# A graph network kernel on one core: products of zeros ahead of the first loads, another second product, and the first sums on VectorE

## The chip, the core and the metric

The kernel runs on one core of a Trainium2 chip. The metric is device time in microseconds of one execution, the median over several. Beside the timed runs there is one profiled execution, and all views of the profile are of that one. The engines are TensorE (PE; its weight loads are shown as PEld), VectorE (DVE), ScalarE (ACT), GpSimd (POOL) and SyncE (SP), which issues most DMAs here.

## The reference

128 graphs of 128 nodes with 512 features each pass two layers, all in fp32. With `x` of shape (128, 128, 512) and `adj` of (128, 128, 128):

```
deg = sum(adj, -1)
agg = (adj @ x) / max(deg, 1e-6)
x   = layernorm(x + relu(concat(x, agg) @ W.T))          # layer 0, W is (512, 1024)
h   = relu(adj @ (x @ W1) + b1)
h   = relu(adj @ (h @ W2) + b2)
x   = layernorm(x + adj @ (h @ W3) + b3)                 # layer 1, W1..W3 are (512, 512)
```

## The kernel before, in words

Four graphs make a quad; there are 32 quads. Within a quad a product of 512 rows by a 512x512 weight is cut into 2x2 blocks and done in Strassen-Winograd fashion: 7 block products instead of 8, with sums of blocks of the data and of the weight made beforehand by other engines. From the third quad on, the products are cut a second time in the same way (`inner_product`, L617). The first two quads use one level in layer 0 (`product`, L599, four fp32 matmuls of 128x128 by 256 columns; the trace shows each as two records).

The two halves of the first weight are called WB (it multiplies x to give `y`, which `adj` then aggregates, L916) and WA (it multiplies x directly). Both live in the tile `big`. The first quad's transposed x lives in the tile `T1` (in the profile `T`), the second quad's in `xT`. Each holds seven places, one for each of the seven products: places 0, 1, 2, 3, 4, 5, 6 belong to products 1, 7, 6, 5, 2, 4, 3. The operands of products 1 and 2 are raw blocks on both sides. The other five take a sum on at least one side:

- `Data.sums` (L446) makes the places 3, 2, 1 and 6 of x from its four loaded blocks (places 0, 1, 4, 5). By default it asks for GpSimd, with VectorE as a substitute; with `at_end=True` for VectorE alone.
- `Weight.__init__` (L343) loads four blocks of a weight into four places, and `Weight.sums` (L349) makes the other three, on VectorE, and puts a fourth difference in the place of a loaded block.

`wino_a` (L775) issues the first five of the seven products, `wino_b` the last two. The order in `wino_a` is 1, 5, 6, 2, 7. In the first quad (`key[1]` is 0) the copy of product 1, which ScalarE makes, is added to the bank of product 2 by VectorE; in the others the bank is seeded with it.

No instruction is issued where it stands in the program. Each is recorded in `Plan` with an estimated duration, the keys that it reads and writes, and the buffers that it takes. `Plan.deadlines` gives TensorE's operations due times in the order in which they are recorded, and the others due times from those. `Plan.order` then plays the engines in time with the estimates and takes for each engine the most urgent operation that is ready (for TensorE the first ready one of the next 48). So the order of all engines' work, the DMAs on SP's queue included, follows from the recorded order of the products: a load that an earlier product needs gets an earlier due time. What is emitted directly, as the memset of `eps` (L1244), stands ahead of the plan.

Once both halves of the first weight have been used by the first quad, `to_forms` (L377) writes the 49 inner blocks of each to DRAM (`forms`), and from the third quad on `Streamed.parts` (L425) loads the blocks of both halves again into a ring of six buffers, three of them in `big`. The degrees of the first quad go through DRAM on ScalarE's queue (`degrees`, L550): `dd`, then `ah`; the row of degrees also gates the loads of W1, W2 and W3.

Of the kernel before, what the change touches and what calls it, by code (L numbers as in the profile page):

```python
# [14 lines left out]
P = 128  # L15
# [228 lines left out]
def gnn_resnorm_kernel(  # L244
# [15 lines left out]
    nc = tc.nc  # L260
    NG, F = x.shape[0], 512
# [12 lines left out]
    def tile_of(shape, name):  # L274
        return sbuf.tile(shape, F32, tag=name, name=name)

    BANK = [psum.tile([P, 2, H], F32, tag=f"bank{i}", name=f"bank{i}") for i in range(8)]
    S_T = [tile_of([P, 2, H], f"s{i}") for i in range(NS)]
# [7 lines left out]
    AT_T = [tile_of([P, G, P], f"at{i}") for i in range(2)]  # L286
# [22 lines left out]
    def pinned(ins):  # L309
        return tc.keep_in_program_order(ins)  # L310

    def vector(n, emit, reads, writes, shared=False, lead=None):
        plan.op("DVE", 0.06 + 0.00123 * n, emit, reads, writes, shared, lead=lead)
# [4 lines left out]
    def dma(dst, src, reads, writes, size, queue="SP", lead=None):  # L318
        eng = nc.sync if queue == "SP" else nc.scalar
        plan.op(queue, 0.06, lambda: pinned(eng.dma_start(dst(), src())), reads, writes, size=size, lead=lead)  # L320

    def const(v):
        return lambda: v

    def add(eng, n, dst, a, b, reads, writes, op=OP.add, shared=False, lead=None):

        on_vector = lambda: pinned(nc.vector.tensor_tensor(dst(), a(), b(), op=op))  # L327
        if eng == "POOL":
            on_gpsimd = lambda: pinned(nc.gpsimd.tensor_tensor(dst(), a(), b(), op=op))  # L329
            plan.op("POOL", 0.03 + 0.00243 * n, on_gpsimd, reads, writes, True, other=(0.06 + 0.00123 * n, on_vector), lead=lead)  # L330
        else:
            vector(n, on_vector, reads, writes, shared)
# [5 lines left out]
    class Weight:  # L338
# [4 lines left out]
        def __init__(self, name, w, after=()):  # L343
            self.name, self.t, self.ti = name, W_T[name], WI_T.get(name)
            wv = w.rearrange("(h c p) (o n) -> p h o c n", p=P, c=2, o=2)
            for i, j, k in ((0, 0, 0), (0, 1, 3), (1, 1, 6), (1, 0, 4)):
                dma(const(self.t[:, k]), const(wv[:, i, j]), after, [(name, k)], P * 2 * H * 4)

        def sums(self):  # L349
            for d, a, b in ((1, 6, 3), (3, 3, 0), (2, 6, 3), (5, 4, 2)):  # L350
                add(
                    "DVE", F, const(self.t[:, d]), const(self.t[:, a]), const(self.t[:, b]),
                    [(self.name, a), (self.name, b)], [(self.name, d)], OP.subtract, True,
                )
# [156 lines left out]
    X0, X1 = Data("T1", T_T[1]), Data("xT", XT_T)  # L511
# [22 lines left out]
    def load_xt(q):  # L534
        d = xa(q)
        for h in range(2):
            for ms in ((0,), (1,)) if q == 0 else ((0, 1),):
                dma(
                    const(d.t[:, 4 * h + ms[0] : 4 * h + ms[-1] + 1]), const(xT[q][:, h, ms[0] : ms[-1] + 1]),
                    (), d.keys([4 * h + m for m in ms]), P * F * 4 * len(ms),  # L540
                )
# [26 lines left out]
    def bank_ap(s):  # L568
        return BANK[s.index]
# [7 lines left out]
    def copied(p, n=4):  # L577
        s = Slot("s")
        scalar(n * P, lambda: pinned(nc.scalar.copy(quarters_of(s, n), quarters(p, n))), [p], [s])  # L579
        return s  # L580

    def seeded(p, n=4):

        s = Slot("bank", n * P, seeded=True)
        scalar(n * P, lambda: pinned(nc.scalar.copy(quarters(s, n), quarters(p, n))), [p], [s])  # L585
        return s

    def product(p, a, b, k, start, transposed):
        (ta, ka), (tb, kb) = a.block(k), b.block(k)

        def emit():
            for o in range(2):
                for c in range(2):
                    if transposed:
                        lhsT, rhs = tb[:, c, o * P : (o + 1) * P], ta[:, c].rearrange("p g n -> p (g n)")
                    else:
                        lhsT, rhs = ta[:, c, o, :], tb[:, c, :]
                    r = pinned(
                        nc.tensor.matmul(  # L599
                            bank_ap(p)[:, o, :], lhsT, rhs, start=start and o == 0 and c == 0, stop=c == 1,  # L600
                            skip_group_check=True,
                        )
                    )
            return r

        plan.op("PE", 1.728, emit, ka + kb, [p])
# [168 lines left out]
    def wino_a(key, a, b, c00, c11, transposed=False):  # L775

        py, pz = Slot("bank"), Slot("bank")
        product(py, a, b, 1, True, transposed)
        px = seeded(py) if key[1] else Slot("bank")
        s1 = None if key[1] else copied(py)  # L780
        yield
        product(pz, a, b, 5, True, transposed)
        yield
        product(py, a, b, 6, False, transposed)
        s2 = copied(py)
        yield
        product(px, a, b, 2, not key[1], transposed)
        if s1 is not None:
            add("DVE", F, lambda: bank_ap(px), lambda: bank_ap(px), lambda: S_T[s1.index], [px, s1], [px])
        c00(px)  # L790
        yield
        product(py, a, b, 7, False, transposed)
        s3 = copied(py)
        c11(s3, pz)
        yield
        CHAIN[key] = py, pz, s2
# [20 lines left out]
    def rows_a(key, a, b, t):  # L817
        yield from wino_a(key, a, b, copy_to(t, 0, 0), sums_to(t, 1, 1))
# [176 lines left out]
    def seg_h1_a(q):  # L995
        d = data(q, "h1")
        yield from wino_a(("h1", q), data(q, "g1"), W1, lambda p: relu_to(d, 0, p), sums_h1(q, 1, 1), transposed=True)
# [188 lines left out]
    def seg_last(q, m):  # L1186
# [51 lines left out]
        for j, o in enumerate(os):  # L1238
# [2 lines left out]
                [o], [("out", q, m, j)], P * F * 4,  # L1241
            )

    nc.vector.memset(EPS_T, LN_EPS)  # L1244
    load_xt(0)
    WB = Weight("wb", w0T[F : 2 * F])
    X0.sums()
    WB.sums()
    load_adj(0)
    degrees(0)  # L1250
# [146 lines left out]
```

## Time and profile before

| | us |
|---|---|
| median of 3 timed runs | 2249.04 (2248.91 to 2249.4) |
| profiled execution | 2250.41 |
| its span, first to last instruction | 2248.5 |
| first matmul starts | 5.46 |
| last matmul ends | 2242.2 |

The profiled execution is 1.9 us longer than its span, and 1.4 us longer than the median of the timed runs. How to read the views: a line of the timeline gives the start, the length, the engine, the source line, the operation, what is written from what, and how many instructions in a row it merges; in brackets stands the idle time ahead of it and what ended it. In a table of windows each row is a stretch of time from the start of the span, with the busy time of every engine in it and the number of instructions. Matmul records overlap: one lasts longer than the distance to the next, so TensorE's pace is read from the distance of starts, or from the count in a window that is full.

### The profile page before, as it was taken

Reading aid. Unit: us, or ns where it says so; the run is one execution under the profiler, and the core shown is the slowest. Engines: PE = TensorE matmul, PEld = TensorE weight load, DVE = VectorE, ACT = ScalarE, POOL = GpSimd, SP = SyncE. Lnnn points to the kernel's source line nnn. Section 1 sums busy time; section 2 is a strip of 40 time slices with the busy share of each in tenths; the row PEclk is TensorE's granted clock in tenths of the full one; section 3 lists DMA queues with packets and bytes.
Section 4 is the critical chain, followed back from the end, with each engine's and each line's share of the span. In section 5 each row is a group of like instructions: output and inputs, shape, how many; then the busy total and the mean of one; then the engine's idle time right before and its main releaser. Section 6 shows DMA issues by size and latency. Waiting matters only on the chain.

```text
span 2248.5 us, 39986 instructions
## 1 busy us (share of the span) xinstructions
PE 2235.7 (99%) x13624; PEld 1997.9 (89%) x13624; DVE 1534.5 (68%) x3384; ACT 1330.8 (59%) x2619; POOL 1168.4 (52%) x1508
## 2 busy tenths in 40 slices
PE   8999999999999999999999999999999999999998
PEld 7888889898898888998888989889898898888997
DVE  4766667666777667677666766667666777667674
ACT  2456656566565665566665656656566556665565
POOL 0245654556645465554565455654546655455540
PEclk9999999999999999999999999999999999999999
DMA  8453445534455444454444553445534455443431
GB/s 268 125 156 125 149 142 174 175 121 145 130 176 176 127 146 134 159 176 140 139 144 143 178 162 124 147 142 172 176 121 149 129 168 176 124 141 129 153 125 38
DMA packets 206330, 333.14 MB, mean 148 GB/s; under 512 B 27056, under 2 KB 72112, under 8 KB 206128
## 3 DMA queue, kind: packets, MB, share of 16 engines
q1 hardware_dynamic: 205696, 330.19, 46.1%
q8 instruction: 109, 1.79, 0.3%
q14 instruction: 93, 0.76, 0.1%
q10 hardware_dynamic: 432, 0.40, 0.1%
HBM read 290.46 MB, written 40.04 MB: 147 GB/s over the span
## 4 chain that ended last, share of the span: by engine, by line
PE 99%; DVE 0%; DMA 0%; issue 0%; SPq 0%; DVEq 0%; ACT 0%
PE bank L617 57%; PE bank L599 21%; PE bank L916 5%; PE bank L941 5%; PE bank L1029 5%; PE bank L1216 5%; DMA big<-in_w0T_dram 0%; DVE big L327 0%; PE bank L1148 0%; SPq L320 0%; DVE ah L327 0%; DVE end_st L1153 0%; DVEq L1392 0%; DVE bank L327 0%; DVE T L327 0%
## 5 line engine op out<-in xcount | busy, mean ns | idle before, releaser
L579 ACT COPY s<-bank 128x384 f32<-128x384 f32 (+1 forms) x567 | 306.6, 541 | 320.6 <-PE bank L617 172.3
L599 PE MATMUL bank<-T,w 128*128 128x256 f32 x1792 | 416.9, 379 | 0.0
L599 PEld LDWEIGHTS bank<-T,w 128*128 128x128 f32 x1792 | 333.5, 190 | 67.2 <-issue 28.7
L329 POOL TENSOR_TENSOR T<-T 128x512 f32<-128x512 f32 (+2 forms) x295 | 279.8, 971 | 199.6 <-DVE T L327 113.2
L327 DVE TENSOR_TENSOR v<-bank,s 128x512 f32<-128x512 f32 x240 | 164.3, 684 | 205.1 <-PE bank L617 204.3
L617 PE MATMUL bank<-big,ti 128*128 128x128 f32 (+1 forms) x1470 | 274.2, 320 | 0.0
L329 POOL TENSOR_TENSOR xT<-xT 128x512 f32<-128x512 f32 (+1 forms) x244 | 237.9, 975 | 36.0 <-DVE ti L327 23.6
L585 ACT COPY bank<-bank 128x512 f32<-128x512 f32 (+2 forms) x273 | 144.0, 527 | 180.0 <-PE bank L617 153.4
L617 PEld LDWEIGHTS bank<-big,ti 128*128 128x128 f32 x1470 | 218.4, 191 | 23.8 <-issue 4.3
L617 PEld LDWEIGHTS bank<-w,T 128*128 128x128 f32 x1680 | 218.3, 192 | 17.1 <-issue 7.2
L327 DVE TENSOR_TENSOR T<-T 128x512 f32<-128x512 f32 (+1 forms) x325 | 223.9, 713 | 8.8 <-ACT T L952 5.8
L617 PEld LDWEIGHTS bank<-w,ti 128*128 128x128 f32 x1680 | 216.1, 192 | 15.5 <-issue 7.2
L617 PE MATMUL bank<-w,T 128*128 128x128 f32 x1680 | 226.5, 275 | 0.0
L617 PE MATMUL bank<-w,ti 128*128 128x128 f32 x1680 | 226.5, 275 | 0.0
L617 PE MATMUL bank<-big,T 128*128 128x128 f32 x1680 | 226.4, 275 | 0.0
L617 PEld LDWEIGHTS bank<-big,T 128*128 128x128 f32 x1680 | 218.3, 192 | 7.7
L327 DVE TENSOR_TENSOR row<-bank,s 128x384 f32<-128x384 f32 (+2 forms) x254 | 119.0, 468 | 152.3 <-PE bank L617 124.8
L617 PE MATMUL bank<-ring,xT 128*128 128x256 f32 x840 | 216.7, 380 | 0.0
L617 PE MATMUL bank<-big,xT 128*128 128x256 f32 x840 | 216.7, 379 | 0.0
L329 POOL TENSOR_TENSOR v<-v 128x384 f32<-128x384 f32 (+1 forms) x61 | 69.3, 1136 | 278.9 <-DVE v L327 144.4
L327 DVE TENSOR_TENSOR v<-v 128x512 f32<-128x512 f32 (+1 forms) x299 | 190.7, 645 | 5.3 <-DVE T L327 0.3
L329 POOL TENSOR_TENSOR s<-s,v 128x256 f32<-128x256 f32 (+1 forms) x60 | 51.8, 863 | 255.2 <-ACT bank L1210 140.7
(99 smaller groups left out, 4166.1 us busy)
## 6 DMA issues: line engine op xcount, KB each, us to landing
big<-forms SPq DMA_DIRECT2D x315, 256.0 KB, 3.2
ring<-forms SPq DMA_DIRECT2D x315, 256.0 KB, 3.3
s<-in_x_dram SPq DMA_DIRECT2D x128, 256.0 KB, 5.9
out_dram<-s SPq DMA_DIRECT2D x126, 256.0 KB, 4.0
xT<-in_xT_dram SPq DMA_DIRECT2D x62, 512.0 KB, 5.6
big<-forms SPq DMA_DIRECT2D x105, 128.0 KB, 2.7
ring<-forms SPq DMA_DIRECT2D x105, 128.0 KB, 2.8
ar<-in_adj_dram SPq DMA_DIRECT2D x32, 256.0 KB, 2.6
```

The source lines that it names most:

```text
L327: on_vector = lambda: pinned(nc.vector.tensor_tensor(dst(), a(), b(), op=op))
L329: on_gpsimd = lambda: pinned(nc.gpsimd.tensor_tensor(dst(), a(), b(), op=op))
L579: scalar(n * P, lambda: pinned(nc.scalar.copy(quarters_of(s, n), quarters(p, n))), [p], [s])
L585: scalar(n * P, lambda: pinned(nc.scalar.copy(quarters(s, n), quarters(p, n))), [p], [s])
L599: nc.tensor.matmul(bank_ap(p)[:, o, :], lhsT, rhs, start=start and o == 0 and c == 0, stop=c == 1, skip_group_check=True,)
L617: nc.tensor.matmul(dst, ta(), tb(), start=start and n == 0, stop=True, skip_group_check=True)
L916: nc.tensor.matmul(bank_ap(p), AH_T[:, :, g], y.graph(g), start=False, stop=True, skip_group_check=True)
L941: nc.tensor.matmul(bank_ap(p)[:, c // 2, (c % 2) * P : (c % 2 + 1) * P], u.chunk(g, c), a[:, g, :], start=c == 0, stop=True, skip_group_ch ...
L1029: nc.tensor.matmul(bank_ap(p)[:, g // 2, (g % 2) * P : (g % 2 + 1) * P], s.chunk(g, o), a[:, g, :], start=g == 0, stop=True, skip_group_ch ...
L1216: nc.tensor.matmul(bank_ap(p), a[:, g, :], s.graph(g), start=False, stop=True, skip_group_check=True)
```

## The change

Three edits at the start, of which two are confined to the first quad.

1. A row of zeros (128x128, in a tile that a load fills later) is written by VectorE, and nine fp32 matmuls of it with itself are issued to bank 7 ahead of everything else on TensorE. Nothing reads their result.
2. In the first product of the first quad, key `("y", 0)`, product 2 is recorded second: the order is 1, 2, 5, 6, 7 in place of 1, 5, 6, 2, 7. The four loads of every weight are recorded in places 0, 1, 6, 4 in place of 0, 3, 6, 4, and `Weight.sums` makes place 3 first, from places 1 and 0, and overwrites place 1 instead of place 3. By the planner's due times SP's queue begins with x and WB for product 1, x and WB for product 2, then two blocks of x and two of WB. Before it began with x and three blocks of WB, three blocks of x, and the fourth of WB.
3. The four sums of the first x are asked of VectorE alone.

```diff
@@ Weight
-            for i, j, k in ((0, 0, 0), (0, 1, 3), (1, 1, 6), (1, 0, 4)):
+            for i, j, k in ((0, 0, 0), (0, 1, 1), (1, 1, 6), (1, 0, 4)):
                 dma(const(self.t[:, k]), const(wv[:, i, j]), after, [(name, k)], P * 2 * H * 4)
 
         def sums(self):
-            for d, a, b in ((1, 6, 3), (3, 3, 0), (2, 6, 3), (5, 4, 2)):
+            for d, a, b in ((3, 1, 0), (1, 6, 1), (2, 6, 3), (5, 4, 2)):
@@ wino_a
+        def second():
+            product(px, a, b, 2, not key[1], transposed)
+            if s1 is not None:
+                add("DVE", F, lambda: bank_ap(px), lambda: bank_ap(px), lambda: S_T[s1.index], [px, s1], [px])
+            c00(px)
+
         product(py, a, b, 1, True, transposed)
         px = seeded(py) if key[1] else Slot("bank")
         s1 = None if key[1] else copied(py)
         yield
+        if key == ("y", 0):
+            second()
+            yield
         product(pz, a, b, 5, True, transposed)
         yield
         product(py, a, b, 6, False, transposed)
         s2 = copied(py)
         yield
-        product(px, a, b, 2, not key[1], transposed)
-        if s1 is not None:
-            add("DVE", F, lambda: bank_ap(px), lambda: bank_ap(px), lambda: S_T[s1.index], [px, s1], [px])
-        c00(px)
-        yield
+        if key != ("y", 0):
+            second()
+            yield
@@ before the recording of the work
+    idle = AT_T[1][:, 0]
+    nc.vector.memset(idle, 0.0)
+    for _ in range(9):
+        (nc.tensor.matmul(BANK[7][:, 1, 0:P], idle, idle, start=True, stop=True, skip_group_check=True))
     nc.vector.memset(EPS_T, LN_EPS)
     load_xt(0)
     WB = Weight("wb", w0T[F : 2 * F])
-    X0.sums()
+    X0.sums(at_end=True)
     WB.sums()
```

As the lines move, L916 becomes L924, L941 becomes L949 and L1244 becomes L1256 in the changed kernel; L599 and L617 stay.

## The prediction

> **What bounds the kernel now.** First the page's totals, then TensorE's own waits.
>
> ```profile
> span 2248.5 us, 39986 instructions
> PE 2235.7 (99%) x13624; PEld 1997.9 (89%) x13624; DVE 1534.5 (68%) x3384; ACT 1330.8 (59%) x2619; POOL 1168.4 (52%) x1508
> ```
> ```profile
> PE bank L599 <- DMA big<-in_w0T_dram: 5.5, 1, 5.5
> PE bank L599 <- DVE T L327: 0.8, 1, 0.8
> PE bank L916 <- DVE ah L327: 0.2, 1, 0.2
> ```
> TensorE waits three times in the whole run: 5.5 us for the first loads, 0.8 us after the first product, 0.2 us at 86.8 us. From 10.05 us to the last matmul at 2242.2 us it has no other gap, so nothing after the start can be gained by relieving another engine. The tail (2242.2 to 2248.5) is not touched. Next, the start by windows (columns: busy us and instructions of PE, PEld, DVE, ACT, POOL) and PE's timeline:
>
> ```profile
> 5.46:9.21 3.75, 3.75 (x8) 2.49 (x8) 2.23 (x4) 0.00 (x0) 0.00 (x0) 1.00 1.07 383
> 9.21:10.05 0.84, 0.01 (x2) 0.01 (x1) 0.84 (x3) 0.59 (x1) 0.00 (x0) 1.00 1.06 365
> 10.05:13.93 3.88, 3.88 (x9) 3.16 (x10) 3.88 (x9) 0.00 (x0) 0.00 (x0) 1.00 1.09 372
> 13.93:17.81 3.88, 3.88 (x19) 3.40 (x19) 1.18 (x5) 0.58 (x1) 0.00 (x0) 1.00 1.07 327
> ```
> ```profile
> 5.46 3.75 PE L599 MATMUL bank<-big,T 128*128 128x256 f32 x8 [5.46 <-DMA big<-in_w0T_dram]
> 10.05 4.11 PE L599 MATMUL bank<-big,T 128*128 128x256 f32 x9 [0.83 <-DVE T L327]
> ```
> Two windows of 3.88 us, both full: 9 matmul records in one, 19 in the next. The same shape starts every 0.427 us before about 13.93 us and every 0.2165 us after it. The trace's clock record begins exactly there; the column of the granted clock shows 1.00 earlier too, so the pitch has to be read from the records. A product is 8 records.
>
> **What the start costs.** Record 18 starts at 13.99 us. Starting at 5.46 at full pitch without a gap it would start at 5.46 + 17 x 0.2165 = 9.14. The start costs **4.85 us**: 17 slow records x 0.21 = 3.6, and the rest the gap. That is the ceiling of this change, as far as the profile shows, apart from the 5.46 us until the first data.
>
> [...] half pitch, opening at 13.93, and half clock on record again at 2246.25, 4.1 us after the last matmul. [...] the 32 records of 128x128 at L941 fill 58.68 to 62.25, 0.111 us each. [...] By the trace's own slope, (0.69 - 0.42)/256 elements, 128 elements on top of the 0.06 us of the eps memset make about 0.19 us, an estimate.
>
> **The change, part by part.**
>
> *Zeros.* The memset stands first on VectorE: 0.81 to 1.00. The eps memset behind it moves by 0.19 us; nobody reads it before the first LayerNorm at 52 us. Nine products of 128x128 are 18 records; cold, twice 0.111 is 0.222 each, 4.0 us. They run from about 1.05 to 5.05, inside the 5.46 us of waiting, so they delay nothing: the cover is 0.4 us, which a pitch of 0.245 us would use up. If each weight load stood bare (0.337 cold, plus the matmul: about 0.63) they would end at 12.4. The row of zeros is later filled by a load issued at 11.8 us in the old order, so SP does not wait for TensorE; bank 7's first real product is around 34 us.
>
> *Gate.* Activity then runs from 1.05 on with one hole of about 0.4 us. [...] the gate opens at latest near 7.9 [...]. [...] This is my choice, not shown.
>
> *Second product and loads.* SP's order becomes X and W for product 1, X and W for product 2, then two X, two W: eight issues, as before. By position the landings are 4.63, 5.32, 6.09, 6.81, 7.50, 8.18, 8.86, 9.59. Product 2 has data at 6.81, before product 1 ends in any case. The third product (5) now needs X's sum (loads at 8.18) and W's difference 1-0 (load at 8.86). VectorE's first sum started 0.10 us after its landing and took 0.69: 8.96 + 0.69 + 0.06, so the third product, and all of TensorE behind it, starts at **9.75**. Unbroken it would start at 5.46 + 16 x 0.2165 = 8.92, so 0.83 us stay. With the gate open by 7.1 the slow records hide in this wait; with the gate at 10.52 the third product starts at about 11.45 and the wait is covered instead. The next sums come every 0.65 us: the fourth product (6) needs its last by 10.9 and starts at 11.5, so no gap.
>
> The second product's own addition (VectorE, bank and copied product) moves from 17.5 to about 12.6. It puts 0.7 us ahead of X's last sum and the degree sum; the former is needed at 20, the latter has the chain below. A later sum, of product 7, waits for ScalarE's copy at about 17.3; behind it stand one W difference and the first form sums, which SP stores only after 24 stores of raw forms: nothing.
>
> *Sums by VectorE alone.* In the old trace the four T sums at L327 already ran on VectorE (9.31 to 12.73), and GpSimd starts at 24.03. Same engine, same 0.68 us: nothing.
>
> *Order after that.* The new issue order puts ACT's DMA of the degrees behind the copy of a later product: about 17.3 instead of 15.77, so it lands at about 20.9 instead of 19.40, and SP's third store of forms, which the trace shows released at 19.40, waits with it. Four issues of forms at 0.54 us now stand behind the first x rows, so these land no later than before (42.3 to 46.4). LayerNorm needs them: first L941 at 58.68 moves to about 53, its rows must be in by about 48. Slack 2 us; cost zero to 2. The order of VectorE, ScalarE and GpSimd is the same again after the first quads; TensorE keeps the same kinds of products, with streamed blocks drawn from other buffers of the ring.
>
> *Sum.* 4.85 - 0.83 = **4.0 us** off the profiled execution, 2250.4 to 2246.4 (span 2244.5). The timed median is 1.4 us below the profiled execution; I subtract the same from it: 2249.04 - 4.0 = **2245.0**. 0.2% is 4.5 us, about what a measurement of this kernel can tell from no change; the forecast lies just inside.
>
> **Rivals.**
>
> *A. Forecast*, gate open before the third product: 2244.4 (loads landing 0.6 us earlier) to 2246.4 (1.4 us of new waits). For: the idle time ahead is long enough for 18 records. Chance 0.50.
>
> *B. The gate opens late*, [...] The excess is (opening - 5.46)/2, 1.7 to 3.4 us: gain 3.1 to 1.4, time 2245.9 to 2247.7. [...] Chance 0.23.
>
> *C. More than counted.* [...] the third product's loads come a little earlier. Gain 4.6 to 5.5, time 2243.5 to 2244.4. Against: three runs agree within 0.5 us. Chance 0.18.
>
> *D. Slower.* SP's order of streamed blocks (L428) differs from quad to quad all through the run. If TensorE at L617 waits for one such load per quad, 30 quads multiply it: at 0.14 us each the 4.0 us are gone, at 0.3 us the time is 2249.0 - 4.0 + 9.0 = 2254. For: 840 such loads share one queue. Against: TensorE waits for none of them now, and they land in about 3.3 us. Bare weight loads (zeros until 12.4) belong here too: record 18 at 16.1, 2251. Together 0.09.
>
> **Numbers.** A to C hold 0.91. Faster by over 0.2%: C's 0.18, and 0.15 of A, whose centre is only 0.5 us from the bound: 0.33. Slower by over 0.2%: nearly all of D, 0.08. The rest, 0.59, is within it. The range takes in C's and B's ends and a stall of about 1 us: 2243.4 to 2248.6.
>
> **What would show it.** Right: 18 records of 128x128 from about 1.05 to 5.1; the third product at 9.75 with a wait of under 1 us on VectorE and 0.2165 us pitch there; three or fewer TensorE waits after it; last matmul near 2238.2. Wrong: pitch still 0.427 after 9.75 (B); product 1 later than 5.5 (zeros overrun); new waits at L617 on loads, or at L949 (the old L941) on ScalarE (D, order).

## The result and the profile after

| | before | after |
|---|---|---|
| median of the timed runs, us | 2249.35 (2248.44 to 2252.34, 22 runs) | 2246.95 (2246.15 to 2248.5, 22 runs) |
| profiled execution, us | 2250.41 | 2247.92 |
| its span, us | 2248.5 | 2246.1 |
| product 1 starts (trace) | 5.46 | 5.12 |
| third product starts (trace) | 13.62 | 9.69 |
| last matmul ends (trace) | 2242.16 | 2239.15 |

The ratio of after to before is 0.9987, 95% interval 0.9982 to 0.9993. The medians differ by 2.4 us, the ratio by 0.13%, which is inside 0.2%: no change by the bound of the forecast, though a gain that the interval tells from zero. The forecast was 2245.0 us with a range of 2243.4 to 2248.6. The measured time lies in the range, and the forecast was 1.95 us too low: it had a gain of 4.0 us where 2.4 were measured.

The page's totals of the changed kernel, then TensorE's waits (us in total, times, longest):

```profile
span 2246.1 us, 40020 instructions
PE 2237.6 (100%) x13642; PEld 1999.6 (89%) x13642; DVE 1534.5 (68%) x3389; ACT 1330.3 (59%) x2619; POOL 1163.4 (52%) x1504
```
```profile
PE bank L1255 <- DVE eps L1256: 1.1, 1, 1.1
PE bank L617 <- DMA ring<-forms: 0.3, 1, 0.3
```

Both waits of the start, 5.5 us for the first loads and 0.8 us for VectorE, have left the list. The first line is now the 1.05 us until the zeros are written. The second is new: far into the run TensorE waited for a streamed block (the list leaves shorter waits out). Next TensorE's timeline of the start and its windows (the second runs from the end of the old first product to the old opening of the clock):

```profile
1.05 4.21 PE L1255 MATMUL bank<-at 128*128 128x128 f32 x18 [1.05 <-DVE eps L1256]
5.12 22.07 PE L599 MATMUL bank<-big,T 128*128 128x256 f32 x96
```
```profile
5.46:9.21 3.75, 3.75 (x14) 3.16 (x14) 1.00 (x2) 0.59 (x1) 0.00 (x0) 1.00 1.03 363
9.21:13.93 4.72, 4.72 (x23) 4.00 (x23) 4.72 (x9) 0.52 (x2) 0.00 (x0) 1.00 1.09 373
```

The zeros end at 5.26, after the first product's data is there (the loads landed at 4.98; before at 5.32), so there is no hole at all: 96 records of the first quad follow in one piece, with no bracket of an idle time. From 5.46 to 9.21 us, where 8 records stood before, there are now 14. In the trace the distance of starts drops from 0.427 to 0.2165 us at 7.23 us, where it was 13.93 before. This moment, at which the trace's record of the full clock also begins, is called the opening of the clock (or of its gate) below. From 11 us on TensorE is **4.02 us ahead** of the old trace, record by record, and it still is at 55 us, past the first matmuls behind LayerNorm.

### The profile page after: what moved, and what is told of

Read it like the earlier page. It is cut to its first block, busy times and chain, and to the rows that moved or that the text cites. A ratio compares the mean times of both kernels' runs of the same rounds, so it can differ in the third digit from the quotient of the medians.

```text
span 2246.1 us, 40020 instructions
## 1 busy us (share of the span) xinstructions
PE 2237.6 (100%) x13642; PEld 1999.6 (89%) x13642; DVE 1534.5 (68%) x3389; ACT 1330.3 (59%) x2619; POOL 1163.4 (52%) x1504
## 4 chain that ended last, share of the span: by engine, by line
PE 99%; DMA 1%; DVE 0%; ACT 0%; DVEq 0%; issue 0%
PE bank L617 57%; PE bank L599 21%; PE bank L924 5%; PE bank L949 5%; PE bank L1037 5%; PE bank L1224 5%; DMA at<-in_adjT_dram 0%; PE bank L1255 0%; DMA ring<-forms 0%; DMA big<-forms 0%; PE bank L1156 0%; DVE T L327 0%; DVE ah L327 0%; ACT T L994 0%; DVE end_st L1161 0%; DVEq L1404 0%
## 5 line engine op out<-in xcount | busy, mean ns | idle before, releaser
L599 PE MATMUL bank<-T,w 128*128 128x256 f32 x1792 | 416.5, 379 | 0.0
L599 PEld LDWEIGHTS bank<-T,w 128*128 128x128 f32 x1792 | 333.6, 190 | 67.2 <-issue 28.2
L329 POOL TENSOR_TENSOR T<-T 128x512 f32<-128x512 f32 (+2 forms) x291 | 274.7, 966 | 189.9 <-DVE T L327 83.7
L617 PE MATMUL bank<-big,ti 128*128 128x128 f32 (+1 forms) x1474 | 280.2, 320 | 0.0
L585 ACT COPY bank<-bank 128x512 f32<-128x512 f32 (+2 forms) x273 | 143.8, 527 | 179.1 <-PE bank L617 154.9
L617 PEld LDWEIGHTS bank<-big,ti 128*128 128x128 f32 x1474 | 219.1, 191 | 24.8 <-issue 6.0
L617 PEld LDWEIGHTS bank<-w,T 128*128 128x128 f32 x1680 | 218.4, 192 | 17.2 <-issue 7.2
L617 PEld LDWEIGHTS bank<-w,ti 128*128 128x128 f32 x1680 | 216.1, 192 | 15.5 <-issue 7.2
L617 PE MATMUL bank<-w,T 128*128 128x128 f32 x1680 | 226.7, 275 | 0.1
L617 PE MATMUL bank<-w,ti 128*128 128x128 f32 x1680 | 226.5, 275 | 0.0
L617 PE MATMUL bank<-big,T 128*128 128x128 f32 x1680 | 226.4, 275 | 0.0
L617 PEld LDWEIGHTS bank<-big,T 128*128 128x128 f32 x1680 | 218.3, 192 | 7.7
L617 PE MATMUL bank<-ring,xT 128*128 128x256 f32 x840 | 218.5, 380 | 0.3 <-DMA ring<-forms 0.3
L617 PE MATMUL bank<-big,xT 128*128 128x256 f32 x840 | 218.5, 380 | 0.1
```

The lines of the kernel that those rows point to most:

```text
L599: nc.tensor.matmul(bank_ap(p)[:, o, :], lhsT, rhs, start=start and o == 0 and c == 0, stop=c == 1, skip_group_check=True,)
L617: nc.tensor.matmul(dst, ta(), tb(), start=start and n == 0, stop=True, skip_group_check=True)
```

## The experiments

All leads below are of TensorE's record starts against the trace that the prediction used, positive where the kernel is ahead. "Lead at the start" is taken at record 40 of the real products (15 to 20 us); 160 records later, at about 55 us, it was the same within 0.02 us in every kernel. The first four kernels share 39 timed runs of the kernel before (median 2250.57).

**1. The changed kernel again.** No edit.

> The changed kernel once more, nothing altered. Two theories of the 1.0 us that its profile loses between 130 us and the last matmul (TensorE waiting at L617 for streamed blocks near 366, 568, 854, 991, 1193 and 1618 us). Chance: the issue order leaves several loads 3.3 us between issue and use in the old kernel as well, and some land late in one execution and not in another; then the start is 4.0 us ahead of the old kernel again at 40 us, the waits stand at other places or are gone, their sum is anything from 0 to 1.3 us. Order: the new order makes these loads tighter; then the waits stand at the same places with about the same sum. Span 2245.0 to 2246.5.

Measured: 2247.36 us (2246.18 to 2248.45, 12 runs), ratio 0.9988 (0.9979 to 0.9997). Its profile:

```profile
1.05 4.21 PE L1255 MATMUL bank<-at 128*128 128x128 f32 x18 [1.05 <-DVE eps L1256]
5.16 4.42 PE L599 MATMUL bank<-big,T 128*128 128x256 f32 x16
10.15 17.53 PE L599 MATMUL bank<-big,T 128*128 128x256 f32 x80 [0.58 <-DVE big L327]
```

The start repeats, with one difference: from the fourth on the loads landed about 0.5 us later, so VectorE's difference for the third product ended later and TensorE waited 0.58 us. The clock opened at 6.64 us. The lead at the start is 3.52 us, at the last matmul 2.45. The places where TensorE waits at L617 for a streamed load are others than in the first profile (368, 1615 and 1818 us instead of 366 and 991), while the sum of the loss is about the same (1.07 and 1.01 us), so neither theory is borne out whole. A wait near 2005 us recurs in both (0.12 and 0.18 us); it is for ScalarE (`v`, L645) and not for a load.

**2. The zeros alone**, added to the kernel before:

```diff
+    idle = AT_T[1][:, 0]
+    nc.vector.memset(idle, 0.0)
+    for _ in range(9):
+        nc.tensor.matmul(BANK[7][:, 1, 0:P], idle, idle, start=True, stop=True, ...)
```

> The kernel before with the memset and the nine products of zeros alone. No recorded operation changes, so every engine's order is that of before. Theory (two halves that need each other): the clock opens near 7.2 us, the first product ends near 8.2, and the second still waits for VectorE's sum until about 10.0; from there full pitch. TensorE is then 1.9 us ahead of the kernel before from 20 us on, and the time 1.9 us shorter. Rival (the zeros are the whole change): 4 us ahead. Rival (zeros do not count as activity): 0.

Measured: 2249.68 us (2249.16 to 2251.96, 12 runs), ratio 0.9999 (0.9991 to 1.0008). TensorE's timeline:

```profile
5.69 2.04 PE L599 MATMUL bank<-big,T 128*128 128x256 f32 x8 [0.43 <-DMA big<-in_w0T_dram]
10.28 19.26 PE L599 MATMUL bank<-big,T 128*128 128x256 f32 x88 [2.55 <-DVE T L327]
```

The first product, 3.75 us long before, takes 2.04, and the wait behind it grows from 0.83 to 2.55: in the old order the sums that the second product needs come no earlier. Lead at the start 1.67 us, which comes from the second product's full pitch. The clock opened at 5.84, 0.15 us behind a hole of 0.43 us (5.26 to 5.69). That a hole of this size would not keep the clock shut was the author's estimate in the prediction; it held in this run.

The time did not follow as expected: 1.9 us less were forecast, the medians differ by 0.9, and the ratio can't be told from 1. Probably this is in part because many executions of the kernel before start as well as this one by themselves (the profiles of numbers 5 to 11 show one). Two of the 12 timed runs here, 2251.43 and 2251.96 us, also have a granted clock of 0.998 on record where all others have 0.999 or 1.000; whether the clock closed once more in their wait of 2.55 us isn't shown.

**3. The order and the sums, without zeros**, and the same once more as number 7:

```diff
-    idle = AT_T[1][:, 0]
-    nc.vector.memset(idle, 0.0)
-    for _ in range(9):
-        nc.tensor.matmul(BANK[7][:, 1, 0:P], idle, idle, start=True, stop=True, ...)
```

> The changed kernel without the memset and the products of zeros: loads, second product and sums as changed. Theory: TensorE starts cold at 5.1 to 5.5 us, two products keep it busy without a gap, and the clock opens [...] anywhere from 8.6 to 12.3. TensorE is 2.1 us ahead of the kernel before from 20 us on (1.3 to 3.1). Rival (the order is the whole change): 4 us ahead.

> The changed kernel without the zeros a second time. Its first trace had the clock open at 8.0 us, [...] and lay 3.7 us ahead. Theory (zeros only narrow the draw): opening anywhere between 8.0 and 11.4, so 2.0 to 3.7 us ahead of the profile on record at 40 us. Rival (zeros are worth nothing, the opening is tied to the start of the program): 8.0 again and 3.7 ahead.

Measured: 2247.42 us (2246.29 to 2248.3, 12 runs), ratio 0.9988 (0.9979 to 0.9996); the second profiled execution 2246.84. The first two products follow each other, in the first profile and in the second:

```profile
5.05 15.29 PE L599 MATMUL bank<-big,T 128*128 128x256 f32 x63 [5.05 <-DMA big<-in_w0T_dram]
```
```profile
5.18 15.15 PE L599 MATMUL bank<-big,T 128*128 128x256 f32 x59 [5.18 <-DMA big<-in_w0T_dram]
```

Same kernel, same kind of start, but up to about 20.3 us, where both views end, 63 records fit into the one and 59 into the other. The clock opened at 8.00 and at 9.59, which is 2.95 and 4.41 us after the first product began, with leads of 3.74 and 2.89 us. So the opening isn't tied to the start of the program, nor to that of the first product. The expectation of number 3 had put the lead at 1.3 to 3.1 us and missed it: it rested on an opening between 8.6 and 12.3 us, the author's estimate, and the one at 8.00 came earlier.

**4. The change with the first sums left to GpSimd or VectorE:**

```diff
-    X0.sums(at_end=True)
+    X0.sums()
```

> The changed kernel with the first x's sums asked of GpSimd by default again. In its issue order GpSimd takes the first of these sums, and VectorE has the addition to the second product's bank ahead of the first weight difference. Theory: the third product then waits for the second one's end (about 9.5 to 9.7), that addition (0.7) and the difference (0.7), and starts near 11.1 in place of 9.69: TensorE is 2.6 us ahead of the kernel before at 40 us, 1.4 us of the gain is lost. Rival (the prediction's: the sums run on VectorE anyway, the edit is worth nothing): 4.0 us ahead as with it.

Measured: 2248.02 us (2247.06 to 2248.79, 12 runs), ratio 0.9989 (0.9981 to 0.9998). TensorE's timeline and, below it, VectorE's and GpSimd's first work in the same stretch:

```profile
11.27 17.50 PE L599 MATMUL bank<-big,T 128*128 128x256 f32 x80 [1.55 <-DVE big L327]
```
```profile
9.84 0.70 DVE L327 TENSOR_TENSOR bank<-bank,s 128x512 f32<-128x512 f32 x1 [8.83 <-PE bank L599]
10.45 0.68 DVE L327 TENSOR_TENSOR big<-big 128x512 f32<-128x512 f32 x1
```
```profile
9.00 1.26 POOL L329 TENSOR_TENSOR T<-T 128x512 f32<-128x512 f32 x1 [8.56 <-DMA T<-in_xT_dram]
```

With the new loads the planner gives the first sum of x to GpSimd, where it takes 1.26 us in place of 0.69. VectorE, free of it, takes up the addition of the second product, and the weight's difference (`big`) stands behind that until 11.13, so TensorE waits 1.55 us. Lead at the start 2.43 us, 1.1 to 1.6 us less than in the two profiles of the changed kernel. Not all of that is the order of VectorE's work: in this trace the load that the difference needs landed at 9.58 (8.81 and 9.32 in those two), so the difference could hardly have begun before 9.7, and it began at 10.45. That leaves about 0.8 us for the third edit here, an estimate; the medians of the same series differ by 0.66 us (2248.02 - 2247.36).

**5, 6, 9, 10 and 11. The kernel before, unchanged.** Its timed runs spread over 4 us, those of the changed kernel over 2.3. Of 87 executions of it, 40 lie under 2250 and 47 above, with one peak from 2249.0 to 2249.5 (22 runs) and one from 2251.5 to 2252.0 (15 runs). More profiles were to show what makes the difference.

> The kernel before once more, for its trace. The timed runs of it fall into two groups, near 2249 and near 2251.5 us; its profile on record (2250.4) belongs to the upper one. Theory: [...] the clock opens between 8.5 and 9.7, the next nine records run at full pitch, and the time is in the lower group, 1.9 us ahead of the profile on record from 20 us on. If not, it opens between 13.0 and 15.2 and the time is in the upper group. Rival (waits for streamed blocks set the groups): TensorE stands within 0.5 us of the old profile at 40 us and the difference arises later, at L617.

> The same kernel a second time[...]: clock opening between 8.5 and 9.7 with a time near 2249, or between 13.0 and 15.2 with a time near 2251.5. Rival as there.

> The kernel before, unchanged, for one more profile. Its times fall into two groups (about 2248.4 to 2249.9 and 2250.0 to 2252.5 us) and all three of its profiles so far are of the upper one (openings at 13.0 to 15.0 us). Theory 1, [...] in the lower group [...] the gate opens between 8.5 and 10.5 us instead of 13.0 to 15.2, and the first fast records save about 1.9 us, so that TensorE runs 1.2 to 2.2 us ahead of the old profile at 40 us. Expected of such a look: a time of 2248.4 to 2249.9, opening 8.5 to 10.5. Theory 2, chance in the streamed loads: the groups differ by waits at L617 or by the last stores; then a look under 2249.9 opens after 13 us all the same, and is level with the old profile at 40 us. A look over 2250.0 has to open after 13 us in theory 1.

> The same as the look above, once more, so that a profile of the lower group is likely to be among them (about half of all runs are). Theory 1: a time under 2249.9 goes with an opening at 8.5 to 10.5 us and a lead of 1.2 to 2.2 us at 40 us over the old profile; a time over 2250.0 with an opening at 13.0 to 15.2 us and a lead within 0.7 us of none. Theory 2: openings always after 13 us, and the time is made at L617 or at the end.

> The same once more. Theory 1: under 2249.9 with an opening at 8.5 to 10.5 us, over 2250.0 with one at 13.0 to 15.2 us. Theory 2: no relation between the opening and the time.

| time, us | clock opens (trace) | lead at the start | lead at the last matmul |
|---|---|---|---|
| 2250.41 (the profile of the prediction) | 13.93 | 0 | 0 |
| 2251.03 | 15.0 | -0.57 | -0.66 |
| 2250.96 | 13.67 | 0.10 | -0.45 |
| 2251.41 | 14.36 | -0.22 | -0.93 |
| **2249.26** | **9.75** | **1.96** | 1.29 |
| 2252.90 | 14.80 | -0.41 | -2.36 |

The two timelines of TensorE that tell it, first of 2249.26 us, then of 2252.9:

```profile
5.39 3.75 PE L599 MATMUL bank<-big,T 128*128 128x256 f32 x8 [5.39 <-DMA big<-in_w0T_dram]
9.99 19.26 PE L599 MATMUL bank<-big,T 128*128 128x256 f32 x88 [0.84 <-DVE T L327]
```
```profile
5.43 3.75 PE L599 MATMUL bank<-big,T 128*128 128x256 f32 x8 [5.43 <-DMA big<-in_w0T_dram]
10.00 21.62 PE L599 MATMUL bank<-big,T 128*128 128x256 f32 x88 [0.82 <-DVE T L327]
```

Up to 10 us they are the same: the first product at half pitch, then a wait of 0.8 us. After that the same 88 records take 19.26 us in the one and 21.62 in the other. In the first of them the clock opened at 9.75 us, within the wait, and was open when the second product began; in the other it opened at 14.80, 4.8 us after the second product had begun. The work up to 10 us is the same in both, so what sets the moment isn't shown.

The five profiles that opened after 13 us are all over 2250 us, and the one that opened before 10 is under it. A single profile of the lower group is little, but something in the timed runs differs with the group, too. Of the 60 timed runs of the kernel before beside numbers 1 to 8 and 12, 23 lie under 2250 us, and 12 of these have a granted clock of 1.000 on record, the others 0.999; of the 37 above, 2 have 1.000. In the two traces of the prediction and the result the only half clock on record lies at the end of the run (from 2246.25 us on before, from 2242.96 after). If waits at L617 alone made the groups, there would be no plain reason for the granted clock to differ between them. That the lower group is a start that by chance was already half repaired is the author's reading of this and of the one profile; the timed runs don't show when their clock opened.

The slowest one shows the other source of spread. Its waits contain

```profile
PE bank L617 <- DMA ring<-forms: 0.9, 2, 0.5
```

and its lead fell by 1.95 us between 55 us and the end. In the other profiles of the kernel before, the fall is between 0 and 0.72 us. This is the same kind of loss that the changed kernel shows (1.01 and 1.07 us in its two profiles), in a kernel whose order was not changed. Nor is the trace that all leads refer to free of it: number 7 gained 0.86 us on it in this stretch.

**8 and 12. Room for the streamed blocks.** The two streamed loads for which TensorE waited in the new profile, at 366 and 991 us, took 3.68 and 3.49 us from issue to landing, where the 840 loads of this kind take 3.1 us in the median. Two attempts to give such loads more room, each on top of the change:

```diff
-    DMA_US, DMA_RATE = 2.0, 0.22e6
+    DMA_US, DMA_RATE = 2.6, 0.22e6
```
```diff
-SIZES = 9, 3, 6, 6
+SIZES = 9, 3, 6, 7
```

> The changed kernel with the planner's fixed part of a load at 2.6 us in place of 2.0 (DMA_US). Its tightest loads of streamed blocks have 3.3 us from issue to use, which is what 2.0 us and 256 KB at its rate come to, and these are the ones that TensorE waits for when they take 3.4 to 3.8. Theory: planned with 3.85 us, the tight ones vanish, no waits at L617, and the last matmul keeps the whole lead that TensorE has at 260 us (3.5 to 4.3 us ahead of the old profile, in place of 2.4 to 3.0): 0.5 to 1.5 us faster than the changed kernel. Rival (the room is set by the six ring buffers and not by the plan): the same 3.3 us and the same waits, or a stall of TensorE where the plan finds no block in time.

> The changed kernel with seven buffers for streamed blocks instead of six (SIZES 9, 3, 6, 7), which moves the planner's order after the start too. In the changed kernel's profile 8 of 840 streamed loads had landed less than 0.5 us before their use, and 1.0 us of TensorE's lead of 4.0 was lost at such loads. Theory 1, a buffer comes free too late for these few loads: a seventh one lets each of them be issued earlier; fewer than 4 loads stay under 0.5 us, no wait of over 0.1 us for a load at L617, and the lead at the last matmul stays as it is at 200 us; a time of 2245.8 to 2246.6 us, about 0.5 to 1 us under the changed kernel. Theory 2, the planner spends the buffer (it gives a load a due time and fills what room it has): as many tight loads as before, at other places, and the same time within 0.4 us of the changed kernel (2246.6 to 2247.4), or slower, to 2250, if the new order meets waits for banks, as with the shorter transfer estimate.

Measured: with the longer transfer estimate 2257.47 us (2256.02 to 2259.0, 9 runs), ratio 1.0031 (1.0021 to 1.0041); with the seventh buffer 2294.8 us (2294.11 to 2295.84, 5 runs), ratio 1.0198 (1.0184 to 1.0212). TensorE's waits in mid-run with the largest sums, with the longer estimate and then with seven buffers:

```profile
PE bank L617 <- ACT bank L701: 1.5, 3, 0.6
```
```profile
PE bank L617 <- ACT bank L585: 13.2, 20, 0.7
PE bank L924 <- DVE u L327: 6.4, 9, 0.7
```

No forecast of the time came true in either. With seven buffers the list has no wait for a load at L617 any more, as theory 1 had it, but the planner, given another number, orders the whole run anew, and the new order meets waits for banks (L585) and for VectorE (L924): TensorE is 44 us behind the old trace at the last matmul. With the longer estimate TensorE's lead at the start was 3.92 us, and at the last matmul it was 7.8 us behind; there the largest sum is for a bank too (L701), and waits for loads remain (`ring` 0.7 us, `big` 0.6). Nothing follows for the change, except that neither constant could be moved here without a new order of the whole run.

## Why the prediction was right or wrong

**Zeros.** Right: 18 records from 1.05, the last ending at 5.26 (predicted 5.05), and product 1 not held up.

**Gate.** Right: openings at 7.23 and 6.64 (predicted at latest near 7.9). That the clock would be open so soon was the author's estimate, from no run. Of the holes ahead of an opening the profiles show this much: behind the one of 0.43 us in number 2 the clock opened within 0.15 us; in the kernel before, with its wait of 0.80 to 0.85 us behind the first product, it opened within that wait in one profile (9.75) and 3.6 to 4.9 us after it in the other five (13.67 to 15.0). Whether the wait kept it shut in these isn't shown.

**Third product.** Right: predicted 9.75 (the terms as written add up to 9.71), measured 9.69. The load behind the weight's difference landed at 8.81 (8.86 was reckoned), and the difference ran from 8.90 to 9.60, with the sum of x ahead of it at 8.14.

**"Sums by VectorE alone: nothing."** Wrong, by about 0.8 us (number 4's own trace and the medians) to 1.6 us (against the first profile). The step looked at the old trace, where these sums ran on VectorE anyway, and took it that they would stay there. Number 4 shows that with the new order of loads they don't. The 4.0 us were right all the same, because the sum placed the operation where the third edit puts it.

**Order after that (0 to 2 us).** Zero: the lead of 4.02 us is the same before and after LayerNorm's first rows.

**The sum on the profiled execution: 4.0 predicted, 2.5 measured.** The start gave its 4.02. Two terms were missing. (a) TensorE lost 1.01 us of it at L617. The waits at 366 and 991 us (0.30 and 0.12 us) are for streamed loads, the one at 2005 us (0.12) is for ScalarE, and smaller ones make up the rest. Rival D had the mechanism, but not the measure: it reckoned with one wait per quad. Since the kernel before loses 0 to 1.95 us in this stretch from one profile to the next, and number 7, with the new order, gains 0.86, this looks like chance rather than a cost of the new order, as far as these profiles tell. (b) "The tail is not touched" failed. From the last matmul to the end of the span it is 6.35 to 6.37 us in all six profiles of the kernel before and in numbers 2 and 4, but 6.99 and 6.93 in the two of the changed kernel, and 6.66 and 6.65 in the two without zeros. In the changed kernel the instructions up to the last store are the same to 0.02 us; the stores land later. The DMA view from 2236 us on (KB each, median us to landing), before and then after:

```profile
out_dram<-s SPq DMA_DIRECT2D x3, 128.0 KB, 2.1
out_dram<-s ACTq DMA_DIRECT2D x1, 128.0 KB, 2.3
```
```profile
q14 instruction: 1, 0.01, 0.1%
...
out_dram<-s SPq DMA_DIRECT2D x3, 128.0 KB, 3.0
out_dram<-s ACTq DMA_DIRECT2D x1, 128.0 KB, 3.2
```

In the changed kernel a transfer of instructions falls among the last stores; in the old one there is none in this stretch. That the one delays the others is argued from their meeting in both profiles of the changed kernel; no run moved that transfer alone. Without zeros the stores land in 2.1 us as before, and the 0.3 us come later: VectorE's last instruction but one (a DRAIN) ends at 6.44 us after the last matmul instead of 5.95. The reason isn't shown. Together 4.02 - 1.01 - 0.64 = 2.37 us, which is the difference of the spans; the remaining 0.1 of the 2.5 us lies around the span.

**"I subtract the same from it."** This is the step that put the forecast 2 us low. The profiled execution stood 1.4 us above the timed median, and the text took that for a constant of profiling. There is no such constant: in numbers 2, 3, 4 and 12 the profiled execution lies within 0.11 us of the median. By the reading above it was the difference of two kinds of start. Of the 22 timed runs of the kernel before, 16 lie under 2250 us, with the profile 2249.26 in their midst; its start was 1.96 us better than that of the profile in which the gain was counted. For those runs, if they start as it does, the change could take only 4.02 - 1.96 = 2.06 us from the start: 2249.04 - 2.06 = 2247.0, against 2246.95 measured. That the two agree so closely is luck, since the sum leaves out the tail and the losses at L617. No rival asked whether the kernel before starts better in many executions than in its profile. Rival C looked for a larger gain alone, and held against it that three timed runs agreed within 0.5 us; all three were of the lower group. With the other mix of the first series here (24 of 39 runs of the kernel before over 2250) the same change is worth more: 2250.57 - 2247.36 = 3.2 us. The tail's 0.6 us and the losses at L617 are of the size of what is left over. The two profiled executions of the changed kernel (2247.92 and 2248.45 us) stand 1.0 and 1.1 us above the medians of its timed runs, so a typical run probably loses less at these two places than they show; at which of them stays open.

**What the parts are worth.** They overlap. In leads at the start: zeros alone 1.67, order and sums alone 2.89 to 3.74, all together 3.52 to 4.02 us. In medians of one series the version without zeros is level with the full change (2247.42 and 2247.36), so no timed run shows a gain from the zeros once the order is changed. No version here beats the changed kernel.

## What to carry to other kernels

A profile is one execution: before a gain that hangs on when the clock opens (9.75 to 15.0 us in six profiles of one kernel here) is subtracted from a median, see whether the timed runs fall into groups, and to which of them the profile belongs; three runs that agree can all lie in one group. Work that fills a wait at the start and an order that removes the wait buy the same thing, and are worth less together than their sum. When an edit names the engine of an operation, it costs nothing only if the planner would choose that engine in the changed order too.

## What was not expected of the hardware

- The clock opened at no fixed moment of a kernel: in the six profiles of the kernel before at 9.75 us and from 13.67 to 15.0, in the two of the changed kernel at 7.23 and 6.64, in the two without zeros at 8.00 and 9.59. What sets the moment isn't shown.
- Once open, the clock stayed open over number 2's wait of 2.55 us: the 88 records behind it take 19.26 us, as long as the same records of the profile of 2249.26 us. Behind the last matmul half clock comes on record after 4.09 us in the kernel before and after 3.81 us in the changed one. The stretch at full clock between opening and end is 2232.32 us long in the first trace and 2235.73 in the second.
- With nothing but products of zeros from 1.05 to 5.26 us the clock opened at 5.84 in number 2, 0.15 us after the first real product began. In the same kernel without them it opened at 9.75 us at the earliest, in six profiles.
- The tail of a kernel can change by 0.6 us, in both profiles of the changed kernel, though its last instructions and stores do not: the stores landed in 3.0 and 2.9 us (median of the three on SP's queue) instead of 2.1.
